# One decoder layer: the first batch's recurrence on its own, context tiles spread behind the first heads, and the router's logits of fourteen batches on GpSimd

## Chip, cores and metric

The kernel runs on one core of a Trainium2 chip. The metric is device time in microseconds (us) of one execution; lower is better. Engines are named as in the profile: PE is TensorE's matrix multiply and PEld its weight load, DVE is VectorE, ACT is ScalarE, POOL is GpSimd, SP is SyncE, whose queue issues most of the DMAs.

## What is computed

Inputs are 16 batches of 256 tokens of width 256, and for each batch 77 context rows. All arithmetic is float32. The reference, cut to what matters:

```python
# 1. recurrence ("rec"), per batch
h  = silu(causal_conv4(x @ in_w.T + in_b))              # 256 -> 512 channels
xp = h @ xp_w.T + xp_b                                  # -> 2 x 16
a  = exp(-exp(xp[..., :16])); b = silu(xp[..., 16:]) * h.sum(-1)
state_t = state_{t-1} * a_t + b_t                       # scan over 256 tokens
x  = layernorm(x + states @ out_w.T + out_b)
# 2. attention, 8 heads of width 128, over 77 context rows and the 256 tokens
cn = layernorm(ctx) * g_media + b_media;  ln = layernorm(x) * g_lat + b_lat
q = ln @ Wq + bq;  k, v = split(concat([cn, ln]) @ Wkv + bkv)
x = layernorm(x + softmax(q k^T / sqrt(128)) v @ Wo + bo)
# 3. router and experts: 8 experts, top 2, 512 rows per expert
dot = x @ emb.T                                         # (tokens, 8): the logits
# the two largest of the 8 are kept and softmaxed; each expert takes its first
# 512 tokens; out = relu(tok @ w1[e].T) @ w2[e].T, weighted, summed per token
x = layernorm(x + expert_output)
```

## The kernel before

**One program, its order given by a planner.** The code lists steps; a scheduler then orders each engine's instructions, earlier steps first where several are ready, and every engine runs its own list strictly in order. An instruction that waits therefore holds up all that stand behind it on its engine. `tc.issue_after(ins)` puts instructions of an engine behind a given one.

**Prologue.** `rec_in(pr, c)` (L282) takes one 128-channel chunk of a pair of batches: two float32 products on PE into a PSUM bank of tag "mm" (two of these), a bias on ACT into `hp`, a convolution of one tensor_scalar and three scalar_tensor_tensor on DVE into `cv`, tanh on ACT, one more DVE step into `hs`. `rec_state` (L307) makes decay and input of the scan for several batches at once, on 128 partitions, and scans on DVE. `rec_add` (L357) multiplies by out_w and adds x; `rec_out` (L371) normalizes into `xs` (layernorm: statistics on DVE, the power -1/2 on POOL by `rsqrt`, L132). `context(t)` (L382) takes one of ten 128-row tiles of the context: norm, turn on PE, scale on ACT into `kvc`, 16 products for the values, which go to DRAM (`vc`). `prep_norm`, `prep_keys`, `prep_sums`, `prep_values` (L420 to L500) make a batch's transposed tokens and its values, the latter by seven block products from sums (`wsum`, `tsum`). Before: all four chunks of the first pair, contexts 0 to 4, batch 0's preparation, contexts 5 to 9; then the heads.

**Heads.** 16 x 8 heads in a software pipeline. In turn i PE runs `head_kq(i)` (products pk, pq), the steps hung on that head, `head_out(i-2)` (po), the scores of head i (s), and `head_turn(i-1)` (transposes pa, pb of the probabilities), then "late" steps. Between the scores of i and its turn lie DVE's maximum (nm, L529), ACT's exponentials (p, L533), DVE's reciprocal (rs, L535) and two products by it (pn, L538); after the turn DVE copies pa (ptt, L552).

**Steps on the heads** (L774 to L830): with batch b run, for the batch before it, `project` (heads 2, 3: output product, bias on POOL into `xb`, sum on DVE into `yb`, norm), `turn_tokens` (head 5: four PE transposes, a DVE copy, L632), `score_experts` (head 6: the logits, eight PE instructions with 8 columns and a DVE copy, L652), `choose` (head 6: top 2, some 14 small DVE operations), `dispatch` (head 7: running counts, then four indirect DMAs from POOL into `xg`), `settle` (head 7, POOL). The recurrence of later pairs, in chunks, and the preparation of batch b+1 also hang there. Batch 15 runs the router steps of batch 14 two heads earlier.

**Experts.** After the last head, nine groups of rows through two products each (L971, L996), a gather of the other expert's row, the last norm, and indirect DMAs to the output. In the last group, DVE adds the gathered row first and takes the product's bank afterwards (L1004).

Of the kernel before, what the change touches and what calls it, by code (L numbers as in the profile page):

```python
# [18 lines left out]
P = 128  # L19
# [4 lines left out]
J = S + M  # L24
# [14 lines left out]
def decoder_layer(  # L39
# [22 lines left out]
    bo,  # L62
    embT,
# [67 lines left out]

    def rsqrt(v, n, rows, name):  # L132
        r = small.tile([P, n], F32, tag="r", name=f"r{name}")
        G.tensor_tensor(r[:rows], v[:rows], nhalf[:rows, 0:n], ALU.pow)
        return r
# [46 lines left out]
    emb_s = wpool.tile([P, DC, E], F32, tag="emb", name="emb_s")  # L182
    wsum = wpool.tile([P, 4, 512], F32, tag="wsum", name="wsum")
# [8 lines left out]
    def load_xT(pr):  # L192

        xTs[pr] = aw.tile([P, DC, PT], F32, tag="xT", name=f"xT{pr}")
        nc.sync.dma_start(xTs[pr], xT[:, pr * PT : (pr + 1) * PT].rearrange("(c p) t -> p c t", p=P))
# [9 lines left out]
    nc.sync.dma_start(inw, in_wT.rearrange("(c p) f -> p c f", p=P))  # L205
    load_xT(0)
    for dst, src in ((inb, in_b), (cw, conv_w), (cb, conv_b), (gm, g_media), (bm, b_media)):
        nc.scalar.dma_start(dst, src)
    NCT = -(-B * M // P)

# [3 lines left out]
    ctx_flat = ctx_in.rearrange("b m d -> (b m) d")  # L214
    ctxs = []
    for t0, t1 in ((0, 1), (1, 5), (5, NCT - 1), (NCT - 1, NCT)):
        c = b2.tile([P, t1 - t0, D], F32, tag="v" if t1 - t0 == 4 else "ctx", name=f"ctx{t0}")
        rows = ctx_rows(t0)
        nc.sync.dma_start(
            c[0:rows, 0 : t1 - t0, :], ctx_flat[t0 * P : t0 * P + rows * (t1 - t0), :].rearrange("(t p) d -> p t d", p=rows)  # L220
        )
        ctxs += [c[:, i, :] for i in range(t1 - t0)]

    xpw = aw.tile([P, NI, 2 * NST], F32, tag="xpw", name="xpw")
    nc.sync.dma_start(xpw, xp_wT.rearrange("(c p) s -> p c s", p=P))
    half = aw.tile([P, 2 * NST], F32, tag="half", name="half")
    G.memset(half, 0.5)
# [4 lines left out]
    for g in range(0, P, 2 * NST):  # L232
        nc.sync.dma_start(xpb[g : g + 2 * NST], xp_b)
        nc.sync.dma_start(outw[g : g + NST], out_wT)
        nc.sync.dma_start(outw[g + NST : g + NST + 1], out_b)
# [7 lines left out]
    wkv_d = wkv.rearrange("(c p) f -> p c f", p=P)  # L243
    nc.sync.dma_start(wkv_s[:, :, INNER:], wkv_d[:, :, INNER:])
    load_x(0)
    load_x(1)
    for dst, src in ((gl, g_lat), (bl, b_lat), (bq_s, bq), (bkv_s, bkv)):
        nc.sync.dma_start(dst, src)
    nc.sync.dma_start(wkv_s[:, :, 0:INNER], wkv_d[:, :, 0:INNER])
    nc.sync.dma_start(wq_s, wq.rearrange("(c p) f -> p c f", p=P))  # L250
# [7 lines left out]
    def load_rest():  # L258
        nc.sync.dma_start(wo_s, wo.rearrange("(h p) f -> p h f", p=P))
        nc.sync.dma_start(bo_s, bo.broadcast_to([P, D]))  # L260
        nc.sync.dma_start(emb_s, embT.rearrange("(c p) e -> p c e", p=P))
    zero = wpool.tile([P, DX], F32, tag="zero", name="zero")
# [17 lines left out]
    hss, sums, yss, xs, stats = {}, {}, {}, {}, {}  # L280

    def rec_in(pr, c):  # L282

        if c == 0:
            hss[pr] = aw.tile([P, NI, PT], F32, tag="hs", bufs=2, name=f"hs{pr}")
            if pr > 0:
                sums[pr] = aw.tile([P, PT], F32, tag="sums", bufs=2, name=f"sums{pr}")
        ph = bank(f"ph{pr}_{c}")
        for k in range(DC):
            T.matmul(ph, lhsT=inw[:, k, c * P : (c + 1) * P], rhs=xTs[pr][:, k, :], start=(k == 0), stop=(k == DC - 1))  # L290
        hp = a2.tile([P, PB, KC - 1 + S], F32, tag="hp", name=f"hp{pr}_{c}")
        G.memset(hp[:, :, 0 : KC - 1], 0.0)
        A.activation(
            hp[:, :, KC - 1 :], ph.rearrange("p (b s) -> p b s", b=PB), AF.Identity, bias=inb[:, c : c + 1]
        )
        cv = a2.tile([P, PB, S], F32, tag="cv", name=f"cv{pr}_{c}")
        V.tensor_scalar(cv, hp[:, :, 0:S], cw[:, c, 0:1], cb[:, c : c + 1], ALU.mult, ALU.add)
        for k in range(1, KC):
            V.scalar_tensor_tensor(cv, hp[:, :, k : k + S], cw[:, c, k : k + 1], cv, ALU.mult, ALU.add)  # L299
        z = cv.rearrange("p b s -> p (b s)")  # L300
        th = a2.tile([P, PT], F32, tag="th", name=f"th{pr}_{c}")
        A.activation(th, z, AF.Tanh)
        V.scalar_tensor_tensor(hss[pr][:, c, :], th, 1.0, z, ALU.add, ALU.mult)
        if c > 0 and pr > 0:
            G.tensor_tensor(sums[pr], hss[pr][:, 0, :] if c == 1 else sums[pr], hss[pr][:, c, :], ALU.add)

    def rec_state(first, last):  # L307

        n = last - first + 1
        members = [first + g % n for g in range(4)]  # L310
        rows = [slice(g * 2 * NST, (g + 1) * 2 * NST) for g in range(4)]
# [16 lines left out]
        parts = [sums[b // PB] for b in members] if first else None  # L328
        for c in range(1 if first else NI):
            for g, (b, r) in enumerate(zip(members, rows)):  # L330
# [3 lines left out]
                    rhs=parts[g][:, tokens(b)] if first else hss[0][:, c, tokens(b)],  # L334
                    start=(c == 0),
                    stop=(first > 0 or c == NI - 1),
                )
        zb = aw.tile([P, S], F32, tag="zb", name=f"zb{first}")
        V.tensor_scalar(zb, px[:, 0:S], xpb, None, ALU.add)
        dec = aw.tile([P, S], F32, tag="dec", name=f"dec{first}")  # L340
        A.activation(dec, zb, AF.Exp)
        A.activation(dec, dec, AF.Exp, scale=-1.0)
        pp = bank(f"pp{first}")
        T.matmul(pp[:, 0:S], lhsT=perm, rhs=zb, start=True, stop=True)
        bs = aw.tile([P, S], F32, tag="bs", name=f"bs{first}")
        A.activation(bs, pp[:, 0:S], AF.Tanh, scale=0.5)
        V.scalar_tensor_tensor(bs, bs, 1.0, pp[:, 0:S], ALU.add, ALU.mult)
        V.tensor_tensor(bs, bs, sg[:, 0:S], ALU.mult)
        ys = a2.tile([P, S], F32, tag="ys", name=f"ys{first}")
        V.tensor_tensor_scan(ys, dec, bs, 0.0, ALU.mult, ALU.add)  # L350
        V.tensor_scalar(ys, ys, one_row, None, ALU.add)
        for b, r in zip(members[0:n], rows):
            yss[b] = ys[r, :], outw[r, :]
# [3 lines left out]
    def rec_add(b):  # L357

        pys = [bank(f"py{b + i}") for i in range(PB)]
        for h in range(2):  # L360
            for i in range(PB):
# [4 lines left out]
        for i in range(PB):  # L366
# [15 lines left out]
    def context(t):  # L382
# [3 lines left out]
        layernorm(zc, zc, 1, rows, f"c{t}")  # L386
        pt = bank(f"pt{t}")
# [10 lines left out]
        if t % 2 == 0:  # L398
            stages[t // 2] = b2.tile([P, 2, INNER], F32, tag="ot", name=f"vc{t}")
        vc = stages[t // 2][:, t % 2, :]  # L400
        for half in range(2):
            f0 = half * 512
            pv = bank(f"pvc{t}_{half}", ("pk", "pq", "pa", "po")[(2 * t + half) % 4], 1)
# [8 lines left out]
            if half == 0:  # L412
                V.tensor_copy(vc[0:rows, f0 : f0 + 512], pv[0:rows])
            else:
                A.copy(vc[0:rows, f0 : f0 + 512], pv[0:rows])
        nc.sync.dma_start(vc_d[t * P : t * P + rows, :], vc[0:rows, :])

    stages = {}

    def prep_norm(b):  # L420

        r2 = again(*stats.pop(b), f"z{b}")
        zl = b2.tile([P, 2, D], F32, tag="zl", name=f"zl{b}")
# [20 lines left out]
    def weight_sums():  # L444
# [3 lines left out]
        V.tensor_tensor(t(0), w(0, 1), w(0, 0), ALU.subtract)  # L448
        V.tensor_tensor(t(1), w(1, 1), w(0, 1), ALU.subtract)
        V.tensor_tensor(t(2), w(1, 1), t(0), ALU.subtract)  # L450
        V.tensor_tensor(t(3), w(1, 0), t(2), ALU.subtract)
# [70 lines left out]
    def head_softmax(b, h):  # L522
# [7 lines left out]
        p = b2.tile([P, 2, J], F32, tag="p", name=f"p{b}_{h}")  # L530
# [5 lines left out]
        pn = b2.tile([P, 2, J], F32, tag="pn", name=f"pn{b}_{h}")  # L536
        for ic in range(2):
            V.tensor_scalar(pn[:, ic, :], p[:, ic, :], rs[:, ic : ic + 1], None, ALU.mult)  # L538
        pns[b, h] = pn
# [36 lines left out]
    def project(b, i):  # L576
# [20 lines left out]
        y = b2.tile([P, 2, D], F32, tag="yb", name=f"yb{b}")  # L597
        V.tensor_tensor(y.rearrange("p i d -> p (i d)"), pws.pop(b), xb.rearrange("p i d -> p (i d)"), ALU.add)  # L598
        norms[b] = layernorm(xs[b], y, 2, P, f"b{b}")
# [19 lines left out]
    def settle(b):  # L619

        r2 = again(*norms.pop(b), f"o{b}")
        o = b2.tile([P, 2, D], F32, tag="yb", name=f"o{b}")
# [29 lines left out]
    def score_experts(b):  # L652
# [13 lines left out]
        V.tensor_copy(lgs[b].rearrange("p t e -> p (t e)"), pl[:, 0 : GT * E])  # L666

# [108 lines left out]

    def behind(b, h, f, *args):

        late_steps[b, h].append((f, args))

    for h in range(H):
        at(0, h, clear, h)
    at(1, 0, clear, H)
    for b in range(B):
        nb = b + 1
        new_pair = nb % PB == 0 and nb < B
        if b > 0:
# [3 lines left out]
            at(b, 5 - early, turn_tokens, b - 1)  # L791
            at(b, 6 - early, score_experts, b - 1)
            at(b, 6 - early, choose, b - 1)
            at(b, 7 - early, dispatch, b - 1)
            at(b, 7, settle, b - 1)
        if new_pair:
# [4 lines left out]
            at(b, 1, rec_add, nb)  # L801
            at(b, 1, rec_out, nb)
            at(b, 2, prep_norm, nb)
            at(b, 3, rec_out, nb + 1)
            at(b, 3, prep_keys, nb)
            at(b, 3, prep_sums, nb)
            for n, h in enumerate((4, 6, 7)):
                at(b, h, prep_values, nb, n, False)
                behind(b, h, prep_values, nb, n, True)
        elif nb < B:  # L810
# [7 lines left out]
    at(0, 0, load_xT, 1)  # L818
# [360 lines left out]
```

## Time and profile before

| | before |
|---|---|
| median of 3 runs, us | 1200.22 (1199.39 to 1200.71) |
| profiled execution, us | 1201.09 |
| its span, first to last instruction, us | 1199.3 |
| its mean granted TensorE clock | 0.991 |
| PE / DVE / ACT / POOL busy, us | 1152.6 / 748.6 / 485.4 / 312.3 |
| first product of the first head (L512) starts at | 89.38 us |
| last product of an expert ends at, about | 1191 us |

The profiled execution is 1.8 us longer than its span, and 0.9 us above the median. Views of it: the page (busy time by engine, 40 slices of the span, the chain that ended last, the costliest groups of instructions); the groups by line; the table of stretches (busy time of each engine in windows, with the granted clock, the DMA share and GB/s); the waits; and the timeline (start, duration, engine, line, operation, what it writes and reads, how many merged, and in brackets the idle time of the engine before it and what ended that). A float32 product shows as two PE instructions. Matmuls are pipelined, so a row's duration overlaps the next row's start by about 0.2 us; the distance from start to start is what a row takes from PE.

### The profile page before, as it was taken

What the parts mean: (1) busy time and instruction counts of PE and PEld (TensorE: products, weight loads), DVE (VectorE), ACT (ScalarE), POOL (GpSimd) and SP (SyncE); (2) the same over time, 40 slices, a digit from 0 to 9 for tenths busy, and PEclk for the clock granted to TensorE, in tenths of its full rate; (3) what the DMA queues carried; (4) which work ended last, traced back from release to release, by engine and by line L of the source; (5) the groups of instructions that cost most, each with busy time, mean ns of one, the idle gap of its engine ahead of it and who ended that gap; (6) DMA issues with size and microseconds to landing.
All of it is one profiled execution on the core that took longest, in us unless ns stands there. A gap on an engine that the chain in (4) does not pass through costs nothing. (4 is left out here: it accounts for less than half of the span.)

```text
span 1199.3 us, 15750 instructions
## 1 busy us (share of the span) xinstructions
PE 1152.6 (96%) x5134; PEld 827.8 (69%) x5134; DVE 748.6 (62%) x2226; ACT 485.4 (40%) x1273; POOL 312.3 (26%) x560
## 2 busy tenths in 40 slices
PE   6789999999999999999999999999999999999996
PEld 2337676767777767767777777677777778876664
DVE  5535768596646765874658576756465645666665
ACT  2125434444344434443435343534343433423331
POOL 2200132222221332222213222232122211225554
PEclk8899999999999999999999999999999999999999
DMA  6760001001000110010000000010001000125762
GB/s 207 226 188 11 19 20 37 28 10 56 18 29 9 35 36 23 9 46 18 15 10 23 29 21 9 4 29 4 20 14 45 14 9 3 30 92 171 182 182 85
DMA packets 45402, 60.37 MB, mean 50 GB/s; under 512 B 7813, under 2 KB 35438, under 8 KB 45320
## 3 DMA queue, kind: packets, MB, share of 16 engines
q1 hardware_dynamic: 38552, 50.13, 13.6%
q0 software_dynamic: 6048, 9.22, 3.1%
q8 instruction: 41, 0.67, 0.2%
q14 instruction: 41, 0.34, 0.1%
q10 hardware_dynamic: 720, 0.01, 0.0%
HBM read 36.07 MB, written 30.78 MB: 56 GB/s over the span
## 5 line engine op out<-in xcount | busy, mean ns | idle before, releaser
L564 PE MATMUL po<-ptt,v 128*128 128x256 f32 (+1 forms) x768 | 190.0, 382 | 6.3 <-DVE ptt L552 6.3
L564 PEld LDWEIGHTS po<-ptt,v 128*128 128x128 f32 (+1 forms) x768 | 142.7, 190 | 58.7 <-issue 25.7
L529 DVE TENSOR_REDUCE nm<-s 128x2 f32<-128x666 f32 x128 | 108.3, 846 | 117.1 <-PE s L527 117.1
L512 PE MATMUL pk<-kvt,wkv_s 128*128 128x333 f32 x512 | 164.9, 444 | 0.0
L527 PE MATMUL s<-kt,qt 128*128 128x333 f32 x512 | 164.3, 442 | 0.0
L572 ACT ACTIVATE ot<-po,bkv_s 128x256 f32<-128x256 f32 x128 | 60.8, 475 | 218.9 <-PE po L564 218.7
L533 ACT ACTIVATE p<-s,nm 128x333 f32<-128x333 f32 x256 | 135.4, 535 | 33.7 <-DVE nm L529 32.5
L517 PE MATMUL pq<-kvt,wq_s 128*128 128x256 f32 x512 | 131.2, 378 | 0.0
L512 PEld LDWEIGHTS pk<-kvt,wkv_s 128*128 128x128 f32 x512 | 91.1, 191 | 45.0 <-issue 22.0
L527 PEld LDWEIGHTS s<-kt,qt 128*128 128x128 f32 x512 | 96.4, 188 | 31.3 <-ACT qt L519 0.5
L517 PEld LDWEIGHTS pq<-kvt,wq_s 128*128 128x128 f32 x512 | 96.7, 189 | 30.2
L582 PE MATMUL pw<-wo_s,ot 128*128 128x256 f32 x512 | 115.8, 379 | 0.0
L553 ACT COPY ptt<-pb 77x256 f32<-77x256 f32 x128 | 47.1, 368 | 168.2 <-PE pb L550 168.2
L582 PEld LDWEIGHTS pw<-wo_s,ot 128*128 128x128 f32 x512 | 97.0, 190 | 13.2
L538 DVE TENSOR_SCALAR pn<-p,rs 128x333 f32<-128x333 f32 x256 | 97.8, 416 | 3.8
L760 POOL DMA_INDIRECT xg<-xs,sidx x64 | 66.4, 1038 | 88.7 <-DVE sidx L757 68.0
L550 PEld LDWEIGHTS pa<-ident,pn 128*128 128x128 f32 x512 | 63.6, 141 | 34.8 <-DVE pn L538 6.8
L552 DVE COPY ptt<-pa 128x512 f32<-128x512 f32 x128 | 87.1, 680 | 0.6 <-PE pa L550 0.6
L596 POOL TENSOR_TENSOR xb<-xs,bo_s 128x256 f32<-128x256 f32 x30 | 19.9, 683 | 244.1 <-DVE yb L598 244.1
L550 PE MATMUL pa<-ident,pn 128*128 128x128 f32 x512 | 78.3, 274 | 2.6 <-DVE pn L538 2.6
L514 ACT ACTIVATE kt<-pk,bkv_s 128x333 f32<-128x333 f32 x128 | 69.0, 539 | 19.9 <-PE pk L512 19.6
L299 DVE SCALAR_TENSOR_TENSOR cv<-hp,cw,cv 128x512 f32<-128x512 f32 x96 | 71.8, 751 | 1.9
(231 smaller groups left out, 1670.0 us busy)
## 6 DMA issues: line engine op xcount, KB each, us to landing
v<-vc SPq DMA_DIRECT2D x16, 308.0 KB
vc<-vc SPq DMA_DIRECT2D x9, 512.0 KB
xg<-zero SPq DMA_DIRECT2D x34, 131.0 KB
xe<-xg SPq DMA_DIRECT2D x8, 524.0 KB
xT<-in_xT SPq DMA_DIRECT2D x8, 512.0 KB
xt<-in_x_in SPq DMA_DIRECT2D x16, 256.0 KB
out<-o SPq DMA_DIRECT2D x16, 256.0 KB
w<-in_w1T SPq DMA_DIRECT2D x8, 512.0 KB
```

Source lines behind the costliest of these rows:

```text
L299: V.scalar_tensor_tensor(cv, hp[:, :, k : k + S], cw[:, c, k : k + 1], cv, ALU.mult, ALU.add)
L512: T.matmul(pk[:, 0:J], lhsT=wkv_s[:, k, f], rhs=kvt[:, k, :], start=(k == 0), stop=(k == DC - 1))
L514: A.activation(kt, pk[:, 0:J], AF.Identity, bias=bkv_s[:, h : h + 1])
L517: T.matmul(pq[:, 0:S], lhsT=wq_s[:, k, f], rhs=kvt[:, k, 0:S], start=(k == 0), stop=(k == DC - 1))
L527: T.matmul(s[:, ic, 0:J], lhsT=qt[:, ic * P : (ic + 1) * P], rhs=kt, start=True, stop=True)
L529: V.tensor_reduce(nm, s[:, :, 0:J], AX.X, ALU.max, negate=True)
L533: A.activation(p[:, ic, :], s[:, ic, 0:J], AF.Exp, bias=nm[:, ic : ic + 1], accum_out=sm[:, ic : ic + 1])
L538: V.tensor_scalar(pn[:, ic, :], p[:, ic, :], rs[:, ic : ic + 1], None, ALU.mult)
L550: T.transpose(dst[0:jn, c0 : c0 + P], pn[:, ic, j0 : j0 + jn], ident)
L552: turned = V.tensor_copy(ptt[:, 0:2, :], pt01.rearrange("p (j i) -> p j i", j=2))
L564: T.matmul(po[:, 0:S], lhsT=vs[b][0:jn, jc, h * DH : (h + 1) * DH], rhs=ptt[0:jn, jc, :], start=(jc == 0), stop=(jc == 2),)
L582: T.matmul(pws[b][:, i * D : (i + 1) * D], lhsT=ot[:, h, i * P : (i + 1) * P], rhs=wo_s[:, h, :], start=(h == 0), stop=(h == H - 1),)
```

## The change

Three groups of edits.

- **The first batch alone.** `rec_in`, `rec_state` and `rec_add` take one batch (256 columns) for batches 0 and 1; batch 0's chunks, state and output run in the prologue with contexts 0 to 4 between them (their norms all ahead, `context_norm`). Batch 1's recurrence hangs on heads 0 to 4 of batch 0, its values on heads 5 to 7. Contexts 5 to 9 run as late steps of heads 0 to 4; these use the "mm" banks and write their values in two halves through the buffers of `xb` and `x2`. Loads are reordered to match: half of xT and the halves of inw first, the value half of wkv ahead of the small tables, five small tables moved to ACT's queue, three of the four copies of the small state tables moved into `load_rest`. The four `wsum` subtractions move from DVE to POOL.
- **The router's logits.** For batches 0 to 13 `turn_tokens` and `score_experts` go. POOL instead multiplies the tokens by a broadcast copy of the expert embeddings (`emb_b`, a new 1 MB load) and halves the sums down to 32 wide: per batch four parts, one on each of heads 4 to 7, each of a product of 1024 elements per partition and sums of 512, 256 and 128. One DVE reduction ends it (`score_end`), with `choose`, behind the turn at head 0 of the batch after; `dispatch` moves to that batch's head 2. The parts are ordered on POOL behind the factors of later batches (`prep_factors`, split off `prep_norm`).
- **Buffers.** tanh is written into `hp`; pn is written over p (three buffers of p instead of two and two); `yb` is written over `xb`; `zl` has one buffer. The last expert's third and fourth products use banks of their own. The second pair's chunks of each four move from heads 3, 4, 5, 7 to 2, 3, 5, 6.

The core of the diff:

```diff
+    def score_part(b, i, g):
+        if i == 0 and g == 0:
+            parts[b] = b1.tile([P, GT, E, W], F32, tag="x2", name=f"part{b}")
+        x = xs[b][:, i, 0:D].unsqueeze(1).broadcast_to([P, EG, D])
+        e = slice(g * EG, (g + 1) * EG)
+        m = b1.tile([P, EG, D], F32, tag="prod", name=f"prod{b}_{i}_{g}")
+        G.tensor_tensor(m, x, emb_b[:, e, :], ALU.mult)
+        n = D // 2
+        while n > W:
+            G.tensor_tensor(m[:, :, 0:n], m[:, :, 0:n], m[:, :, n : 2 * n], ALU.add)
+            n //= 2
+        G.tensor_tensor(parts[b][:, i, e, :], m[:, :, 0:n], m[:, :, n : 2 * n], ALU.add)
+
+    def score_end(b):
+        lgs[b] = small.tile([P, GT, E], F32, tag="lg", bufs=2, name=f"lg{b}")
+        V.tensor_reduce(lgs[b], parts.pop(b), AX.X, ALU.add)
...
-            at(b, 5 - early, turn_tokens, b - 1)
-            at(b, 6 - early, score_experts, b - 1)
-            at(b, 6 - early, choose, b - 1)
-            at(b, 7 - early, dispatch, b - 1)
+            if b == B - 1:
+                at(b, 3, turn_tokens, b - 1)
+                at(b, 4, score_experts, b - 1)
+                at(b, 4, choose, b - 1)
+                at(b, 5, dispatch, b - 1)
+            else:
+                for n in range(4):
+                    at(b, 4 + n, score, b - 1, n // 2, n % 2)
+                settled(b + 1, 0, score_end, b - 1)
+                settled(b + 1, 0, choose, b - 1)
+                at(b + 1, 2, dispatch, b - 1)
...
+            at(b, 2, prep_factors, nb)
             at(b, 2, prep_norm, nb)
             at(b, 3, rec_out, nb + 1)
+            at(b, 3, prep_factors, nb + 1)
...
+        elif b == 0:
+            for h in range(2):
+                at(0, h, rec_in, 0, 2 * h, 1)
+                at(0, h, rec_in, 0, 2 * h + 1, 1)
+            at(0, 2, load_xT, 1)
+            at(0, 2, rec_state, 1, 1)
+            at(0, 3, rec_add, 1, 1)
...
+            for h in range(NCT - FIRST_CTX):
+                behind(0, h, context, FIRST_CTX + h, False)
...
-    rec_in(0, 0)
-    rec_in(0, 1)
-    context(0)
-    rec_in(0, 2)
-    rec_in(0, 3)
-    context(1)
-    rec_state(0, 1)
-    context(2)
-    context(3)
-    rec_add(0)
+    for c in range(NI):
+        rec_in(0, c, 0)
+    for t in range(FIRST_CTX):
+        context_norm(t)
+    context(0, True)
+    rec_state(0, 0)
+    context(1, True)
+    rec_add(0, 1)
+    context(2, True)
     rec_out(0)
+    prep_factors(0)
     prep_norm(0)
+    context(3, True)
     prep_keys(0)
-    context(4)
-    rec_out(1)
+    context(4, True)
     wparts = weight_sums()
     prep_sums(0)
...
-    for t in range(5, NCT):
-        context(t)
     load_rest()
```

## The prediction

> **What bounds the kernel now.** I read the page first, then the table of stretches, then the timeline of PE, and last DVE and POOL side by side. From the page, busy time by engine, PE's 40 slices and its clock:
>
> ```profile
> PE 1152.6 (96%) x5134; PEld 827.8 (69%) x5134; DVE 748.6 (62%) x2226; ACT 485.4 (40%) x1273; POOL 312.3 (26%) x560
> ...
> PE   6789999999999999999999999999999999999996
> ...
> PEclk8899999999999999999999999999999999999999
> ```
>
> PE is full except in the first three slices and the last. The table of stretches (length, then busy us and count of PE, PEld, DVE, ACT, POOL, granted clock, DMA share, GB/s) says how full:
>
> ```profile
> 0.00:30.00 30.00, 19.66 (x43) 7.97 (x44) 17.94 (x48) 8.32 (x14) 7.15 (x46) 0.89 0.64 208
> 30.00:60.00 30.00, 21.46 (x103) 9.68 (x102) 16.88 (x47) 5.29 (x12) 8.73 (x22) 0.83 0.72 226
> 60.00:73.00 13.00, 10.75 (x25) 3.99 (x24) 7.24 (x19) 2.57 (x5) 2.28 (x4) 1.00 0.93 223
> ...
> 349.00:418.00 69.00, 69.00 (x314) 52.21 (x313) 44.57 (x119) 30.44 (x84) 14.31 (x26) 1.00 0.07 21
> ```
>
> In the heads any PE instruction that goes is time that goes, as long as DVE and POOL keep up. Ahead of them PE waits and runs at a lower clock. The timeline of PE shows the router's two steps and what follows each:
>
> ```profile
> 437.56 0.60 PE L649 MATMUL px<-ident,xs 128*128 128x128 f32 x4
> 438.00 1.88 PE L290 MATMUL ph<-xT,inw 128*128 128x512 f32 x4
> ...
> 444.78 0.95 PE L658 MATMUL pl<-emb_s,x 128*128 128x8 f32 x8
> 445.59 0.68 PE L477 MATMUL pv<-wsum,tsum 128*128 128x512 f32 x1
> ```
>
> **Router.** From start to start the turn takes 438.00-437.56 = 0.44 us, the logits 445.59-444.78 = 0.81. Fourteen batches: 14 x 1.25 = 17.5 us off PE. DVE loses two copies (0.69 and 0.17 us) and gains a reduction of 512 elements (about 0.7): nothing.
>
> **POOL's price for it.** Its rows by width: 128 elements 0.45 us, 256 0.68, 512 1.30.
>
> ```profile
> L596 POOL TENSOR_TENSOR xb<-xs,bo_s 128x256 f32<-128x256 f32 x28 | 18.5, 681 | 244.1 <-DVE yb L598 244.1
> L305 POOL TENSOR_TENSOR sums<-sums,hs 128x512 f32<-128x512 f32 x14 | 18.2, 1297 | 24.8 <-DVE hs L303 24.8
> L463 POOL TENSOR_TENSOR tsum<-kvt,tsum 128x128 f32<-128x128 f32 x14 | 6.3, 453 | 1.1
> ```
>
> That is 2.4 ns an element, so 1024 elements are about 2.5 us (my estimate from these rows). A part is 2.5+1.3+0.68+0.45 = 4.9 us, a batch 19.7, all fourteen 276. POOL goes from 312 to 588 busy of some 1180: no bound as a sum, but it is packed into heads 4 to 7, about 29 us of each batch's 60, beside 7 to 9 us already there.
>
> The cost is not POOL's time but what it does to DVE. Timeline rows of both engines:
>
> ```profile
> 135.37 0.61 POOL L432 COPY kvt<-kvc 128x154 f32<-128x154 f32 x1 [1.28 <-PE pq L517]
> 135.95 1.34 POOL L305 TENSOR_TENSOR sums<-sums,hs 128x512 f32<-128x512 f32 x1
> ...
> 135.72 1.75 DVE L538 TENSOR_SCALAR pn<-p,rs 128x333 f32<-128x333 f32 x2
> ```
>
> Two pn take 0.69 us elsewhere; here 1.75: the second ends 0.2 us after POOL's sum, so it stood still through it, while the first got in between two POOL instructions. Maxima and PSUM copies beside POOL keep their length. PE lost nothing there, so 1 us is within the slack. The slack, from the second pn's end to the weight load that reads it (timeline rows, medians of heads 4 to 7): 3.0, 2.5, 4.5, 3.6 us in even batches, 2.8, 2.9, 3.8, 3.0 in odd ones; with the router's PE steps gone, heads 4 and 5 fall to about 2.5 and 2. A head lasts about 7.2 us, so a pn pair meets the 2.5 us product with 0.35 chance, waits 1.25 for it on average, then 1.3 for the next sum before its second half: 1.3 to 3.8 us of delay. Past 2.5 of slack that is half the meetings at 0.65 us: 0.35 x 0.5 x 0.65 = 0.11 us a head; at 2 of slack about 0.25. I take 0.15 x 56 heads = 8 us, and 4 for the 14 recurrence chunks that share these heads, whose five DVE steps also touch SBUF only. Ends: 0, as the sums show, and 1.9 us in each of 56 heads (a pair that always meets the product's start: 2.5+1.3+0.6-2.5) = 106. I take 12, near the low end, since the sums are the nearest row.
>
> SBUF — State Buffer (the Trainium skill, section "SBUF: two separate sides") says of this that the port pair shared by Vector and GpSimd is an exclusive lock for a whole instruction, also against Vector operations with two SBUF inputs. For pn the rows agree; for the convolution they show little (at 241.91 two scalar_tensor_tensor took 1.64 us beside POOL's L624, against 1.50). By the rule in full, each of the 14 chunks could stand behind a whole part, 4.9 us less 2.9 of slack, and the sum would be 28 us later.
>
> **Prologue.** The first head's first product starts at 89.38. By then PE has done, start to start: 16 records of chunks at 0.43 (6.9), ten contexts of 8 x 0.43 + 2 x 0.11 (36.6), seven value products of 0.86 (6.0), keys 0.4, state and output about 3.4: 53.3. So 36.1 us are lost before the heads. The chain that sets it, in rows of the timeline (the products after the last chunk, the scan's end, the output, the keys):
>
> ```profile
> 31.70 1.50 PE L319 MATMUL px<-hs,xpw 128*32 128x256 f32 x24
> 37.72 0.35 DVE L351 TENSOR_SCALAR ys<-ys,one_row 128x256 f32<-128x256 f32 x1
> 44.54 1.13 PE L363 MATMUL py<-outw,ys 32*128 32x256 f32 x8
> 54.21 0.98 DVE L439 TENSOR_SCALAR kvt<-pt,gl,bl 128x256 f32<-128x256 f32 x2
> ```
>
> After the change: the first product needs 0.5 MB in place of the 1 MB that landed at 6.26; it can't be before the first small table (4.36); I take 5.0. Four half chunks: DVE 0.35+4x0.42 = 2.0 us each, 8.1, plus five norms of 1.1 that fill in; before, 13.9 us of such work took 21.9 from the first bias to the last hs. Between 8.1 and 16 I take 11, with 2.5 ahead for the first product and bias: last hs at 18.5. Scan chain 38.07-31.70 = 6.4, output to keys 55.19-44.54 = 10.7 as before: keys at 35.6, and the heads can start. PE has five contexts and the small steps to do meanwhile, about 24 us. Pipeline fill 3: lost 35.6-24+3 = 14.6 against 36.1, so 21.5 saved. Ends: keys at 30 (27 saved) and at 50 (7). What hides the moved work: five contexts, 18 us, stand in heads 0 to 4, where DVE has room (my sum: 60 us of DVE in batch 0's 78 of PE). Batch 1's own state step costs there what L319 to L564 cost at 142.01 to 146.32, some 3 us; local waits of DVE 2 more (0 to 6). Queues: 4.6 MB are asked of SP ahead of the first head, 22 us at the 208 GB/s above, so the loads land before 35; ACT issues nine small loads at 0.5 us before its first bias, done by 5.5; `load_rest` puts the 1 MB of embeddings and nine small loads, 4 us of SP, ahead of xT of pair 1, wanted only at head 4. The sums of weights on POOL, 4 x 1.3, lie under the contexts. If these covers fail, the keys slip with them. Prologue in all: -21.5+5 = -16.5.
>
> **Waits that the new order meets.** In odd batches at head 3 DVE stands behind POOL's factors:
>
> ```profile
> 432.77 0.35 DVE L425 TENSOR_SCALAR zl<-xs,rlz 128x256 f32<-128x256 f32 x1 [2.30 <-POOL rlz L134]
> 433.37 0.69 DVE L538 TENSOR_SCALAR pn<-p,rs 128x333 f32<-128x333 f32 x2
> ```
>
> and PE loses 1.0 (po) and 0.9 (pa) there in seven batches, 12 us. `prep_factors` comes ahead of the sums on POOL, so some goes: -5 (0 to -12). `score_end` makes DVE wait for POOL's last part, with nm, rs and pn of head 0 behind it, and so PE's pa: POOL's 19.7+8 and DVE's blocked stretches against about 32 us from head 4 to there; +2 (0 to 3 x 14 = 42). `choose` and `dispatch` move to heads 0 and 2, where DVE is busy 3.2 of 5.5 and 1.5 of 8.5 us: nothing. In the last group of experts the gather and the chain of DVE and POOL after it stay: -1 to +0.5, taken as 0.
>
> **Sum.** -17.5 -16.5 -5 +12 +2 = -25.0. The profiled execution's 1201.1 becomes 1176; against the median 1200.2, 1175.2. I predict 1175.
>
> **Rivals.** (1) The prologue's chain is not shortened: in-order queues (norms, POOL's powers, loads that wait) push the keys to 50. For it: before, it took 21.9 us for 13.9 of DVE work. Against: the contexts no longer stand before the output on PE (38.07 to 44.54). Time: 21.5-7 = 14.5 later, 1190. (2) POOL's port costs twice as much: 0.55 us in each of 56 heads instead of 14 in all: 31, so 1192, in its upper part level with before. (3) Slower: the same lock in heads 4 to 7, where two operations in a row wait for the long product and POOL so falls behind that `score_end` waits as well; at 1.0 us a head, 56 instead of 14, 1217. It decides from (25+14)/56 = 0.7 us lost per head on. Against it: the sums of 1.3 us beside pn left no gap in PE. For it: 2.5 us is twice that, and the slack is about 2. (4) The edit doesn't do what it says: the planner runs parts early and they stand before a power that DVE waits for; priced like (2).
>
> **How the numbers follow.** Forecast 0.58, own range 1160 to 1187; rival 1 0.12; rivals 2 and 4 0.14, of which 0.04 level; rival 3 0.16. A measurement here tells 0.2%, 2.4 us, from no change. Faster 0.58+0.12+0.10 = 0.80, same 0.04, slower 0.16. With all terms at their good ends the sum is near 1152; 1157 to 1200 leaves out most of rival 3 and a little below.
>
> **What would show it.** Router: no L649 and L658 but for batch 14, PE busy 17 us less there. Prologue: first product of head 0 near 36 to 40 us in place of 89, and a clock of 1.00 from the second stretch on. POOL near 590 busy, a 1024 product near 2.5 us. Port: pn's mean above 416 ns, and idle time of PE's turns released by pn below 12 us. The forecast is wrong if that idle time passes 39 us, if DVE waits long for POOL's parts at head 0, or if the heads start after 50.

## The result, and the profile after

The changed kernel takes 1221.13 us (1220.63 to 1222.29), the kernel before 1199.81 in the same comparison: 1.8% slower, ratio 1.0179 with the 95% interval 1.0162 to 1.0197. 1175 was predicted, between 1157 and 1200; 1221 lies on the side of rival 3, which had put 1217. The profiled execution is 1221.03 us long, its span 1219.3, against 1199.3 before.

The page of the changed kernel, busy time by engine, PE's 40 slices and its clock:

```profile
PE 1148.8 (94%) x4932; PEld 818.6 (67%) x4932; DVE 843.9 (69%) x2233; ACT 488.3 (40%) x1284; POOL 594.4 (49%) x792
...
PE   6899999989999989999999999899999999999996
...
PEclk9999999999999999999999999999999999999999
```

POOL is at 594 as forecast, PE has 202 rows less to do, and the clock no longer starts at 0.8. What is new are 8s amid PE's nines, and 95 us more of DVE. The same stretches as before (length, busy us and count of PE, PEld, DVE, ACT, POOL, then granted clock, DMA share, GB/s):

```profile
0.00:30.00 30.00, 20.24 (x53) 10.09 (x54) 18.51 (x55) 8.03 (x17) 12.92 (x51) 0.94 0.72 230
30.00:60.00 30.00, 26.28 (x79) 13.12 (x78) 15.91 (x42) 8.34 (x18) 5.69 (x14) 1.00 0.64 210
60.00:73.00 13.00, 12.93 (x45) 7.76 (x46) 10.13 (x25) 7.82 (x22) 0.60 (x4) 1.00 0.89 253
...
349.00:418.00 69.00, 65.86 (x295) 48.98 (x294) 50.01 (x132) 29.96 (x81) 34.36 (x42) 1.00 0.08 25
```

Ahead of the heads PE gained: 26.28 busy in the second stretch where it was 21.46. In the heads it lost: 65.86 of 69.00 where it had been busy throughout. The groups by line, forms kept apart, show whose operations grew (count, then busy us and mean ns); the first two lines are of the kernel before, the rest of the changed one:

```profile
L538 DVE TENSOR_SCALAR pn<-p,rs 128x333 f32<-128x333 f32 x256 | 97.8, 416 | 3.8
L299 DVE SCALAR_TENSOR_TENSOR cv<-hp,cw,cv 128x512 f32<-128x512 f32 x96 | 71.8, 751 | 1.9
...
L603 DVE TENSOR_SCALAR p<-p,rs 128x333 f32<-128x333 f32 x256 | 142.4, 592 | 3.2
L753 POOL TENSOR_TENSOR prod<-xs,emb_b 128x1024 f32<-128x1024 f32 x56 | 124.4, 2221 | 2.7
L341 DVE SCALAR_TENSOR_TENSOR cv<-hp,cw,cv 128x512 f32<-128x512 f32 x84 | 88.6, 1055 | 1.7
```

The normalisation of p went from a mean of 416 ns to 592, cv (the convolution's steps with two inputs in SBUF) from 751 to 1055: same instructions, same sizes. So two kinds of DVE operation became longer, and the timeline of one chunk's head shows which of them costs PE time (start, us, engine, line; in brackets the idle time before it and its releaser):

```profile
241.04 3.51 DVE L341 SCALAR_TENSOR_TENSOR cv<-hp,cw,cv 128x512 f32<-128x512 f32 x2
244.48 0.84 DVE L595 TENSOR_REDUCE nm<-s 128x2 f32<-128x666 f32 x1
245.24 1.45 DVE L341 SCALAR_TENSOR_TENSOR cv<-hp,cw,cv 128x512 f32<-128x512 f32 x1
246.61 0.68 DVE L617 COPY ptt<-pa 128x512 f32<-128x512 f32 x1
...
241.52 2.48 POOL L753 TENSOR_TENSOR prod<-xs,emb_b 128x1024 f32<-128x1024 f32 x1
...
244.88 1.25 POOL L756 TENSOR_TENSOR prod<-prod 128x512 f32<-128x512 f32 x1
...
247.43 1.78 PE L629 MATMUL po<-ptt,v 128*128 128x256 f32 x6 [2.75 <-ACT hp L344]
```

Two cv take 1.5 us elsewhere; here 3.51, because the second comes up while POOL's product runs (241.52 to 244.00) and ends 0.55 us after it. The third takes 1.45 in place of 0.75, beside POOL's sum of 512. nm and ptt, which read PSUM, keep their length, but they stand behind cv in DVE's list, and PE's po waits for ptt. (The bracket names the semaphore that came last, hp's tanh at nearly the same moment. po reads ptt, which ends at 247.29, and starts 0.14 us later, as it does at the other heads where it waits for ptt.)

To add this up I took, from the timeline, PE's time between the first products of neighbouring heads, less what its rows need at full rate (shortest distances from start to start: 0.279 us for 333 columns, 0.2155 for 256, 0.429 for 512, 0.109 for a transpose), the state's products and the router's small ones apart. I call the rest "lost in the heads": 20.2 us before, 72.3 after.

| where, after against before | us |
|---|---|
| router's rows gone from PE | -18.3 |
| first product of the first head at 54.11 in place of 89.38; 21.7 of products and 0.6 of state moved into batch 0's heads; 2.5 lost there | -10.5 |
| lost in 14 heads that follow a chunk and share POOL's parts | +38.8 |
| lost at head 4 of odd batches (13.2 before, 20.8 after) | +7.6 |
| lost at head 2 of batches 5 and 9 | +4.2 |
| other heads, and behind the last head | -1.8 |
| sum; the spans differ by 20.0 | +20.0 |

Batches 12 and 14 carry parts but no chunk: none of their heads lost over 0.03 us.

Head 2 of batches 5 and 9 is another case. No product runs on POOL there; in batch 5 DVE works without a gap from 401.56 to 415.39 through a chunk, the reduction of the parts, the choice, the recurrence's output and its norm, and ptt comes late behind these:

```profile
413.05 0.68 DVE L617 COPY ptt<-pa 128x512 f32<-128x512 f32 x1
...
413.88 1.53 PE L629 MATMUL po<-ptt,v 128*128 128x256 f32 x6 [1.82 <-DVE oh L786]
```

### The profile page after: what moved, and what is told of

Its sections match the earlier page's. It is cut to its first block, busy times and chain, and to the rows that moved or that the text cites. A ratio compares the mean times of both kernels' runs of the same rounds, so it can differ in the third digit from the quotient of the medians.

```text
span 1219.3 us, 15390 instructions
## 1 busy us (share of the span) xinstructions
PE 1148.8 (94%) x4932; PEld 818.6 (67%) x4932; DVE 843.9 (69%) x2233; ACT 488.3 (40%) x1284; POOL 594.4 (49%) x792
## 5 line engine op out<-in xcount | busy, mean ns | idle before, releaser
L629 PE MATMUL po<-ptt,v 128*128 128x256 f32 (+1 forms) x768 | 195.1, 389 | 34.2 <-ACT hp L344 16.1
L593 PE MATMUL s<-kt,qt 128*128 128x333 f32 x512 | 170.1, 454 | 0.0
L603 DVE TENSOR_SCALAR p<-p,rs 128x333 f32<-128x333 f32 x256 | 142.4, 592 | 3.2
L753 POOL TENSOR_TENSOR prod<-xs,emb_b 128x1024 f32<-128x1024 f32 x56 | 124.4, 2221 | 2.7
L578 PEld LDWEIGHTS pk<-kvt,wkv_s 128*128 128x128 f32 x512 | 91.2, 191 | 45.3 <-issue 22.5
L593 PEld LDWEIGHTS s<-kt,qt 128*128 128x128 f32 x512 | 99.5, 194 | 32.8 <-issue 3.1
L756 POOL TENSOR_TENSOR prod<-prod 128x512 f32<-128x512 f32 x112 | 117.4, 1048 | 6.7
L341 DVE SCALAR_TENSOR_TENSOR cv<-hp,cw,cv 128x512 f32<-128x512 f32 (+1 forms) x108 | 102.3, 955 | 1.8
L615 PEld LDWEIGHTS pa<-ident,p 128*128 128x128 f32 x512 | 64.6, 143 | 45.3 <-DVE p L603 17.5
L615 PE MATMUL pa<-ident,p 128*128 128x128 f32 x512 | 80.8, 278 | 10.6 <-DVE p L603 10.4
```

Source lines behind the costliest of these rows:

```text
L578: T.matmul(pk[:, 0:J], lhsT=wkv_s[:, k, f], rhs=kvt[:, k, :], start=(k == 0), stop=(k == DC - 1))
L593: T.matmul(s[:, ic, 0:J], lhsT=qt[:, ic * P : (ic + 1) * P], rhs=kt, start=True, stop=True)
L603: V.tensor_scalar(p[:, ic, :], p[:, ic, :], rs[:, ic : ic + 1], None, ALU.mult)
L615: T.transpose(dst[0:jn, c0 : c0 + P], pn[:, ic, j0 : j0 + jn], ident)
L629: T.matmul(po[:, 0:S], lhsT=vs[b][0:jn, jc, h * DH : (h + 1) * DH], rhs=ptt[0:jn, jc, :], start=(jc == 0), stop=(jc == 2),)
L753: G.tensor_tensor(m, x, emb_b[:, e, :], ALU.mult)
```

## The experiments

Theory A: while POOL's long product runs, DVE's operations on SBUF stand still, and what is queued behind them on DVE holds PE. Rivals: B, the other edits cost the time; C, each batch on POOL costs alike, wherever the chunks are; D, the waits for POOL's result cost it; E, the order of POOL's queue; F, DVE has too much to do; G, of a form that is faster by itself.

| run | median, us | ratio to before, 95% | lost in heads, us |
|---|---|---|---|
| changed kernel | 1221.13 | 1.0162 to 1.0197 | 72.3 |
| e1 router on PE | 1187.44 | 0.9869 to 0.9902 | 19.8 |
| e2 old prologue | 1225.72 | 1.0189 to 1.0224 | 68.1 |
| e3 six batches on POOL | 1189.08 | 0.9892 to 0.9925 | 27.6 |
| e4 chunks to heads 0 to 3 | 1220.67 | 1.0150 to 1.0184 | 70.4 |
| e10 chunks to heads 0 to 2 | 1205.57 | 1.0014 to 1.0055 | 51.1 |
| e7 product in four | 1197.40 | 0.9971 to 0.9990 | 47.3 |
| e9 taps (the convolution's steps) read from PSUM | 1180.92 | 0.9828 to 0.9868 | 29.3 |
| e12 the same, router on PE | 1196.07 | 0.9934 to 0.9966 | 23.9 |
| e13 e9 with zl later | 1175.85 | 0.9770 to 0.9798 | 22.5 |
| e5 parts without use | 1292.32 | 1.0723 to 1.0803 | 125.2 |
| e6 fills without use | 1262.00 | 1.0474 to 1.0579 | 97.9 |
| e11 fills for parts | 1259.61 | 1.0451 to 1.0515 | 110.1 |
| e14 e11 with zl later | 1241.99 | 1.0308 to 1.0360 | 90.3 |

### Half of the change at a time: e1 and e2

```diff
-                for n in range(4):
-                    at(b, 4 + n, score, b - 1, n // 2, n % 2)
-                settled(b + 1, 0, score_end, b - 1)
...
+                at(b, 5, turn_tokens, b - 1)
+                at(b, 6, score_experts, b - 1)
+                at(b, 6, choose, b - 1)
+                at(b, 7, dispatch, b - 1)
```

> The changed kernel with the router of all fourteen batches back on PE (turn in head 5, logits and choice in head 6, dispatch in head 7); prologue, context tiles, tiles and recurrence slots stay changed. Theory A (GpSimd's long products hold DVE's chunk operations still, and DVE's queue then holds PE): the 52 us that PE loses more inside the heads go, 17.5 us of router products come back: 1221 - 52 + 17.5 = 1186, between 1180 and 1192. Theory B (the other edits, prologue and schedule, cost the time): the loss stays, 1221 + 17.5 = 1238.

e2 is the other half: router and buffers of the changed kernel, prologue of before.

```diff
-    for c in range(NI):
-        rec_in(0, c, 0)
...
+    rec_in(0, 0)
+    rec_in(0, 1)
+    context(0)
...
+    for t in range(5, NCT):
+        context(t)
```

> The kernel before with the router on GpSimd and the tile edits that make room for it, and with its own prologue: both batches' recurrence and all ten contexts ahead of the first head. Theory A: it has all of the loss in the heads and none of the 14 to 15 us that the prologue gave: 1221 + 15 = 1236, between 1230 and 1241. Theory B: about as before, 1200 less 17.5 to 20 for the router, at most 1200.

e1 measured 1187.4, within 2 us of theory A, and theory B is out. The rest of the change is a gain of 13; the router on POOL is a loss of 34, everything that it brings with it included. e2 at 1225.7 is below A's range: with parts on POOL the new prologue is worth 4.6 us, not 15. In the timelines the first head comes 35.0 earlier than in e2, for 21.7 of work, 4.6 of state products and 4.2 of new losses in the heads. What makes the state's products 4 us shorter in e2 than in the kernel before I did not trace.

### Which batches, and where the chunks stand: e3, e4, e10

```diff
-            else:
+            elif b in (3, 7, 11, 12, 13, 14):
                 for n in range(4):
                     at(b, 4 + n, score, b - 1, n // 2, n % 2)
...
+            else:                                  # eight batches: as in e1
```

> The changed kernel with the router on GpSimd only in the six batches (3, 7, 11, 12, 13, 14) whose heads 4 to 7 hold no recurrence chunk; eight batches on PE. Theory A: PE gains 8 x 1.25 = 10 us of work, and the 39 us lost behind chunks plus 4 at heads (5,2) and (9,2) go: 1221 + 10 - 43 = 1188 at most, and 1186 - 6 x 1.25 = 1179 if these six cost nothing: between 1176 and 1189. Theory C (each batch on GpSimd costs alike, whatever DVE does): 8/14 of 52 go: 1221 + 10 - 30 = 1201.

1189.1 (1185.61 to 1191.05): against C's 1201, and 0.1 above A's range. No head behind a chunk lost more than in e1; what stayed is head 4 of batches 3, 7, 11 and 13 (2.8, 2.8, 2.8, 3.9 against 1.1 in e1), which eats the 7.5 us that six routers free. e3 can't be told from e1.

```diff
-        first = ((1, 1), (1, 3), (1, 5), (1, 7)) if nb == 4 else ((0, 5), (0, 7), (1, 0), (1, 5))
...
+        first = ((1, 1), (1, 2), (1, 3), (1, 3)) if nb == 4 else ((0, 0), (0, 1), (0, 2), (0, 3))
...
-        for c, h in enumerate((2, 3, 5, 6)):
+        for c, h in enumerate((1, 2, 3, 3) if nb == 4 else (0, 1, 2, 3)):
             at(nb - 2, h, rec_in, pr + 1, c)
```

> The changed kernel, all fourteen routers on GpSimd in heads 4 to 7, with all recurrence chunks of pairs 2 to 7 in heads 0 to 3 of the same or a neighbouring batch, and their loads of xT a head or three earlier. Theory A: 39 + 4 us go, some 5 come back because four chunks now stand in heads 0 to 3 together with the projection: 1183, between 1176 and 1192. Theory C: nothing goes: 1221.

Nothing went: 1220.7, C's number. But the losses had moved. They now lie at head 4 of the six batches with such chunks (1, 2, 4, 6, 8 and 10: 13.2, 7.7, 3.0, 4.7, 6.1, 3.0), and the timeline of batch 4 there shows why:

```profile
383.26 3.51 DVE L341 SCALAR_TENSOR_TENSOR cv<-hp,cw,cv 128x512 f32<-128x512 f32 x2
383.75 2.47 POOL L753 TENSOR_TENSOR prod<-xs,emb_b 128x1024 f32<-128x1024 f32 x1
386.69 0.84 DVE L595 TENSOR_REDUCE nm<-s 128x2 f32<-128x666 f32 x1
```

The chunk that hangs on head 3 is convolved when the part of head 4 already runs: the same 3.51 beside the same product. A label in the list of steps is not a time. So e10 leaves head 3 free too, for pairs 4 to 7.

```diff
+            first, second = ((0, 0), (0, 1), (0, 2), (1, 0)), ((1, 2), (2, 0), (2, 1), (2, 2))
```

> The changed kernel, with the chunks of pairs 4 to 7 only moved, to heads 0 to 2 (pair 4: heads 0, 1, 2 of batch 4 and 0 of batch 5; pair 5: head 2 of batch 5 and heads 0, 1, 2 of batch 6; 6 and 7 likewise four batches later), so that none stands in head 3, whose chunk ran beside the part of head 4 in the earlier move. Pairs 2 and 3 stay. Theory A: of the 31 us that PE loses in batches 4 to 10 at heads 2, 4, 6 and 7, about 6 stay where a chunk meets the end of the batch before: 1221 - 25 = 1196, between 1189 and 1206. Theory C (GpSimd's work costs the same wherever the chunks are): 1221.

1205.6, at A's upper end: behind the moved chunks heads 4, 6 and 7 lost nothing, and about 10 us stayed at heads 1 and 2 of these batches, 4 of them at head 2 of batches 5 and 9, as above. C is out: POOL did the same work.

### How long one hold lasts: e7

```diff
-        G.tensor_tensor(m, x, emb_b[:, e, :], ALU.mult)
+        for j in range(EG):
+            G.tensor_tensor(m[:, j, :], xs[b][:, i, 0:D], emb_b[:, g * EG + j, :], ALU.mult)
```

> The changed kernel with the product of 1024 elements as four of 256, 0.7 us each in place of one of 2.2; same sums after it. GpSimd works 0.6 us longer a part. Theory A: an operation of DVE is held for 1.3 at the longest in place of 2.4; a chunk's five steps still meet five or six instructions, so I take half of the 52 us: 1195, between 1185 and 1210. Theory E: GpSimd's queue is 34 us longer in all: 1221 or a little above.

1197.4: 23.7 us went although POOL's products took 162 us in place of 124. The heads behind chunks lose 18 us in place of 39. How long a single POOL instruction lasts counts for more than POOL's time: against E, and against C so far as C goes by POOL's work.

### The other side of the hold: e9, e12, e13

```diff
+        u = ph.rearrange("p (b s) -> p b s", b=PB)             # PSUM
+        A.activation(u, u, AF.Identity, bias=inb[:, c : c + 1])
+        V.tensor_scalar(cv, u, cw[:, c, KC - 1 : KC], cb[:, c : c + 1], ALU.mult, ALU.add)
+        for k in range(KC - 2, -1, -1):
+            d = KC - 1 - k
+            V.scalar_tensor_tensor(
+                cv[:, :, d:], u[:, :, 0 : S - d], cw[:, c, k : k + 1], cv[:, :, d:], ALU.mult, ALU.add
+            )
+        A.activation(u, cv, AF.Tanh)
...
```

> The changed kernel; the chunks of pairs 2 to 7 leave the projection in PSUM: ACT adds the bias in place, the taps read u from PSUM and cv from SBUF, tanh goes back into PSUM, and hs reads it there. Each DVE operation of a chunk has one SBUF input in place of two; its count and length stay, and a bank of PSUM is held some 5 us longer. GpSimd's fill of hp falls away for these chunks. Theory A: the 39 us behind chunks and the 4 at heads (5,2) and (9,2) go, and PE may wait for the held bank, 0 to 10: 1183, between 1176 and 1195. Theory F (DVE has too much to do in heads 4 to 7, and the port has no part in it): no change, 1221.

1180.9, within A's range; POOL's parts are untouched, DVE has as many operations, so F is out for the heads behind chunks. Heads 6 and 7 of batches 2 to 10, and head 4 of the even ones, lose 0.02 each. (F holds at head 2 of batches 5 and 9: e7, e10 and e11 lose the same 2.0 to 2.1 there as the changed kernel. Here it is 0.4 to 0.5; why, I did not trace.) The rows by tile (ns: min, median, max) of the changed kernel and of e9:

```profile
L341 DVE SCALAR_TENSOR_TENSOR cv<-hp,cw,cv x108: 451/752/2725, 12.7 to 785.0; 128x512 f32<-128x512 f32 x84, 128x256 f32<-128x256 f32 x24
L346 DVE SCALAR_TENSOR_TENSOR hs<-hp,cv x36: 412/691/1780, 19.4 to 787.0; 128x512 f32<-128x512 f32 x28, 128x256 f32<-128x256 f32 x8
```

```profile
L360 DVE SCALAR_TENSOR_TENSOR cv<-ph,cw,cv x72: 728/746/750, 152.1 to 746.6; 128x510 f32<-128x510 f32 x24, 128x508 f32<-128x508 f32 x24, 128x506 f32<-128x506 f32 x24
```

With one input in PSUM, not one of 72 operations was over 750 ns; with both in SBUF the longest took 2725. The control, e12, has both edits, this one and that of e1:

> The kernel with the router back on PE and the chunks' taps read from PSUM. Theory A: without GpSimd's parts the taps were not held, so the form with PSUM brings nothing: 1187, between 1184 and 1191. Theory G (this form is faster by itself): 1180 or below, and then the 40 us of the run with both would not all be GpSimd's.

1196.1, 9 us slower than e1 where no difference was expected: the form costs something by itself (4.1 more lost in the heads, 2.4 in state products), so G is out, and what POOL's parts cost through the chunks is rather over than under the 40 us that e9 gained.

In e9 head 4 of odd batches still loses 2.9. The timeline of batch 5 in the changed kernel shows that place:

```profile
435.50 2.43 DVE L491 TENSOR_SCALAR zl<-xs,rlz 128x256 f32<-128x256 f32 x1 [0.97 <-POOL rlz L137]
437.86 0.15 DVE L601 RECIPROCAL rs<-sm 128x2 f32<-128x2 f32 x1
...
435.44 2.35 POOL L753 TENSOR_TENSOR prod<-xs,emb_b 128x1024 f32<-128x1024 f32 x1
...
438.62 0.84 PE L615 MATMUL pa<-ident,p 128*128 128x128 f32 x4 [1.29 <-DVE p L603]
```

The order that lets the parts start right behind the power that zl waits for makes the two start together: zl (0.35 us) takes 2.43, with rs and p behind it.

```diff
-            at(b, 0, prep_norm, nb)
+            settled(b - 1, 6, prep_norm, nb)
```

> The run with taps from PSUM and the router on GpSimd (1181), with one step moved: zl of the next odd batch, which DVE starts at head 4 of odd batches as GpSimd's product of 2.35 us starts and then waits through, comes in head 6 behind the copy of the turned probabilities. Theory A: 7 x (2.88 - 1.14) = 12 us go: 1169, between 1164 and 1176. If the stall moves with it to head 6: 1181.

1175.85, the fastest of all runs, 2.2% below the kernel before; by the medians 5.1 of the 12 us went (by the ratios 7.7: the kernel before ran 2.7 us slower in this comparison than in e9's). Head 4 fell to 1.19 as expected (11.2 us in all), but 4.4 came back, nearly all at heads 6 and 7 of odd batches (0.4 to 0.8 each), where zl now stands; and the first head began 1.9 later, within the spread of these runs (52.5 to 56.3).

### Reads or any use of POOL: e5, e6, e11, e14

e5 is e1 with POOL's parts kept, their last sum written back:

```diff
-        G.tensor_tensor(parts[b][:, i, e, :], m[:, :, 0:n], m[:, :, n : 2 * n], ALU.add)
+        G.tensor_tensor(m[:, :, 0:n], m[:, :, 0:n], m[:, :, n : 2 * n], ALU.add)
```

> The kernel with the router back on PE (1187), and beside it GpSimd still does its parts in heads 4 to 7 of the same fourteen batches; the last sum of a part goes back into its own tile and nothing reads it, so no instruction waits for a part. Theory A (operations of DVE with SBUF operands stand still while GpSimd's long product reads SBUF): the 52 us come back without any wait for a result: 1187 + 52 = 1239, between 1230 and 1246. Theory D (what costs is the wait for the last part ahead of the choice, and the choice and dispatch in heads 0 and 2): at most 1191.

In e6 a part is instead:

```diff
+        for n in (2500, 1450, 800, 560):
+            G.memset(flat[:, 0:n], 0.0)
```

> As the run before, but each part is four fills of 2500, 1450, 800 and 560 elements, which read nothing; by the rows of fills (0.31 us for 262 elements, 0.10 for 8) they take about 2.2, 1.3, 0.75 and 0.55 us, as the product and the sums do, and hold GpSimd's queue as long. Theory A: cv and hs run at their own length, 40 to 52 us go: between 1187 and 1200. Theory E (what GpSimd owes to the heads, the edge of hp, the powers, the sums of hs and of keys, stands behind the parts in its queue): as the run before, 1230 to 1246. The Trainium skill (SBUF — State Buffer, section on who shares what) has the operations with two SBUF inputs contend only with a GpSimd instruction that reads SBUF, and the two-port modes with any: by it the normalisation of p and zl may still be held.

Both were far above either expectation, 1292 and 1262, and not for the reason under test. The waits of PE (us in all, times, longest) of e5, then of e6:

```profile
PE pc L819 <- DVE on L810: 34.5, 11, 4.1
```

```profile
PE pv L543 <- POOL tsum L528: 24.2, 7, 4.5
PE pc L813 <- DVE on L804: 14.3, 7, 2.6
```

With choice and counts of the same batch in heads 6 and 7, beside the parts, PE's counts (pc) wait for the choice; and fills, which depend on nothing, were put in runs ahead of the sums for the values (tsum). These totals say little about A. What the heads say: e5, where no result is waited for, lost 4.7 to 6.1 us at head 4 of batches 2, 6 and 10, behind chunks; e6 lost 0.6 there, as e1 did. So the loss behind chunks needs no wait for a result, against D. In the changed kernel itself DVE's reduction of the parts never waited for POOL; what D has right is the choice, which crowds head 2 of batches 5 and 9. e11 therefore keeps the places and waits of the changed kernel.

```diff
-        G.tensor_tensor(m, x, emb_b[:, e, :], ALU.mult)
...
+        for n in (2500, 1450, 800):
+            G.memset(flat[:, 0:n], 0.0)
+        G.memset(flat[:, 0:430], 0.0)
+        G.memset(parts[b][:, i, e, :], 0.0)
```

> The changed kernel with each part as five fills in the same places, of 2500, 1450, 800, 430 and 128 elements (2.2, 1.3, 0.8, 0.4 and 0.2 us by the rows of fills), the last into the part that is reduced: same tiles, same waits for the result, choice and dispatch as in the changed kernel. It leaves out the logits of fourteen batches, which are zero, so their tokens all choose the same two experts. Theory A: the chunks' steps, cv and hs, run at their own length beside a GpSimd that reads nothing, so 43 us go: 1178, between 1172 and 1192; the 2.9 us at head 4 of odd batches, where zl is held, may stay. Theory E (GpSimd's queue): 1221.

1259.6 in place of 1178. The rows by tile of e11:

```profile
L341 DVE SCALAR_TENSOR_TENSOR cv<-hp,cw,cv x108: 446/750/1493, 11.7 to 806.7; 128x512 f32<-128x512 f32 x84, 128x256 f32<-128x256 f32 x24
L346 DVE SCALAR_TENSOR_TENSOR hs<-hp,cv x36: 409/684/693, 17.3 to 808.7; 128x512 f32<-128x512 f32 x28, 128x256 f32<-128x256 f32 x8
L491 DVE TENSOR_SCALAR zl<-xs,rlz x32: 327/350/7302, 38.9 to 978.9; 128x256 f32<-128x256 f32 x32
```

hs, up to 1780 ns beside reads, is never over 693 beside fills, and cv of 512 has the mean of e1, 757. zl is held more than ever, 7.3 us against 2.4. So there are two kinds of hold: two SBUF inputs stand behind POOL's reads only; one SBUF input to SBUF behind fills too (zl; and p, with a mean of 629 ns against 427 in e1). The time went where zl stands: 63 of the 110 us lost are at heads 4 and 5 of odd batches. Another 31 are at heads 1 and 2 of the even ones.

e14 adds e13's edit, zl in head 6, to e11.

> The run with fills in place of the parts (1260; logits of fourteen batches left out, as there), with zl of the next odd batch moved from head 4 to head 6 as in the run at 1176. In that run cv and hs kept their own length beside the fills (mean 757 and 688 ns), yet PE lost 110 us, 63 of them at heads 4 and 5 of odd batches, where one zl stood behind fills for up to 7.3 us. Theory A (operations with one SBUF source are held by fills as well as by reads, those with two only by reads): the 63 fall to about 9: 1260 - 54 = 1206, between 1194 and 1222. Theory E (GpSimd's queue is what costs with fills): no change, 1260, or the loss moves to head 6.

Heads 4 and 5 of odd batches fell from 63 to 16 us, 47 of the expected 54. But the run only fell by 18: head 1 of the even batches now loses 4.6 to 8.7 each. In all seven of these batches PE's product of tsum starts 0.05 us after POOL's L528 ends, in batch 8 at 613.31. The tile kvt that this sum and those ahead of it read was ready there at 603.39, and POOL ran nothing but fills from then until the first of them at 612.02. So A holds for zl, and with fills, whose order differs from the parts', E holds as well. In the changed kernel head 1 of the even batches loses 0.02.

## Why the prediction was wrong, step by step

- **Router, -17.5.** Right: -18.3. Of L649 and L658 only batch 14's and 15's remain.
- **Prologue, -16.5.** Sign right, size not: -10.5. The keys came at 44.5, between the forecast's 35.6 and rival 1's 50, and the first head at 54.1, past the 50 that the prediction set as a sign against itself: between the two PE had value products and a context to do. So the time lost ahead of the heads fell from 36.1 to 22.5 (35.3 earlier, for 21.7 of products moved) and not to 14.6. Batch 1's state cost 0.6 in place of 3, local waits in batch 0's heads 2.5 in place of 2.
- **Factors, -5.** The edit by itself gives that: in e1 head 4 of odd batches loses 1.1 where it lost 2.05. With parts on POOL the same edit makes the product start beside zl, and the place loses 7.6 us more than before in place of 5 less.
- **Normalisation of p, +8.** Held as described: its mean rose from 416 to 592 ns, 45 us in all. Where no chunk and no zl stood beside it, that cost nothing: batches 12 and 14 lose nothing, and in e9, where p is held as much (mean 619), heads 4, 6 and 7 of the even batches 2 to 10 lose 0.02. There the slack took it in full.
- **Chunks, +4: this is the step that failed.** Measured 38.8. Its nearest row was of two scalar_tensor_tensor beside POOL operations of 0.7 us, which can't show what one of 2.2 does, and the price was taken over from pn: half of its 8 us, with pn's slack. What counted is the slack of what DVE has queued behind the chunk. In the kernel before, ptt ended 1.0 to 4.6 us ahead of its po in heads 4 to 7 of batches 1 to 10; held steps used that up, and PE stood 0.6 to 2.9 us in each of the 14 heads. In six of them PE's clock then fell too, some 1.7 us each or 10 of the 38.8 (last section).
- **The sign for it** was set at the wrong place: PE's idle time at the turns, released by p, is 10.4 us, below the 12 of the forecast. The time was lost at po.
- **`score_end`, +2, and `choose` and `dispatch`, nothing.** DVE never waited for the parts; but the choice at head 0 cost 4.2 at head 2 of batches 5 and 9, where a chunk and the output stand beside it.
- **The rule in full** (the Trainium skill, SBUF — State Buffer, section "SBUF: two separate sides"): an operation with two SBUF inputs contends with a GpSimd instruction that reads SBUF, the two-port modes with any. The prediction priced it at 28 us more and set it aside. For operations with two SBUF inputs e9 and e11 agree with it (at most 750 ns with one input in PSUM, hs at most 693 beside fills, 1780 beside reads). zl and p, held beside fills too, fit its second half, though no row names the mode they ran in. 4 + 28 = 32 was still below the 38.8 measured.
- **Rival 3** had the side and nearly the time, 1217 against 1221, but not the place: not 1.0 us in each of 56 heads, but 1 to 5 in 14 of them, and no wait for `score_end`. That its time came so near is chance.
- **Rival 4** did not occur; the edits do what they say, and POOL's busy time came out at 594 for a forecast of 590.

## What to carry to other kernels

Before work goes to POOL, list DVE's operations by their sources: those with two SBUF inputs stood here through POOL's reads, those from one SBUF tile to another through its reads and its fills, those with one input, or one of two, in PSUM through neither (nm took at most 853 ns and the sums of the values, one input in PSUM and one in SBUF, at most 690, both in the changed kernel and in e11). Then price not the held operation but the first one behind it, in DVE's order, that PE waits for. Where both have to run together, one source in PSUM gained 40 us here, although that form cost 9 by itself, and a product in four instructions 24; moving the chunks to other heads gained 16 (e10) or nothing (e4).

## What the runs showed of the hardware

- Fills hold an operation through several instructions in a row: zl of 0.35 us took up to 7.3, while POOL's longest fill takes 2.2; in e11 one zl of 3.77 us stood through fills of 2.18, 0.20 and 1.31. Beside reads zl got in after one product (2.43 beside 2.35).
- PE's mean granted clock is lower where it stalls more often: 0.995 in e13, 0.988 in the changed kernel, 0.961 in e5. In the changed kernel po and s after a stall of 2.91 us took 2.18 and 2.00 us from start to start (193.43, 195.61, 197.61); without one they take 1.30 and 1.12, so this stall cost some 1.8 us more than itself. The granted clock (last but two of a row) was 0.50 there. It did not fall after every stall: of nine between 1.8 and 2.9 us in the heads, six were followed by 3.4 us at 0.50, and three (1.82, 1.87, 2.75) by 1.00. After equal stalls of 2.75, head 4 of batch 2 lost 4.7 us with the lower clock and head 4 of batch 10 lost 3.0 without.
- A POOL product of 1024 elements takes 2.22 us, four of 256 take 3.0 (0.755 each); a fill of 2500 takes 2.18 to 2.20.

The stretches behind the stall of 2.91 and behind that of 2.75 in batch 10:

```profile
194.00:197.30 3.30, 3.30 (x9) 2.28 (x8) 2.26 (x4) 0.75 (x2) 3.19 (x4) 0.50 0.00 0
...
761.37:764.70 3.33, 3.33 (x17) 2.76 (x18) 3.33 (x5) 1.24 (x3) 3.33 (x5) 1.00 0.23 79
```
